# Attention and a mixture of experts on one core: the residual kept in the output, six weight groups and four output banks

## The chip, the cores and the metric

The kernel runs on one core of a Trainium2 chip. The metric is the time of one execution on the device, in microseconds (us). The core has five engines that work at the same time, each through its own list of instructions in order: PE (matrix products; its weight loads are shown as PEld), DVE (vector work), ACT (activation functions), POOL (general work and transfers that need more than a plain copy) and SP (which only issues transfers). SP, ACT and POOL each issue transfers on a queue of their own.

## The reference, cut to what matters

```python
x = x + layernorm(attn(layernorm(x)))        # 16 x 256 tokens, 256 wide, 16 heads of 128
x = x + layernorm(ffn(layernorm(x)))

def ffn(h):                                  # T = 4096 tokens, E = 64 experts, M = 176
    scores = softmax(h @ gate.T)             # 3 of 8 groups of experts, then 6 of 64 experts
    buf[expert, slot] = h[token]             # 96 slots for each expert; a token past slot 95 shares it
    out = (silu(buf @ Wg.T) * (buf @ Wu.T)) @ Wd.T       # for each expert
    y = sum over the 6 of out[expert, slot] * score
    return y + (silu(h @ Sg.T) * (h @ Su.T)) @ Sd.T      # the shared expert, 352 wide
```

All arithmetic is in float32. The first `x +` is the residual that this change is about: it is needed in attention and again at the very end.

## The kernel before, in words

Tokens lie in 32 chunks of 128, four chunks to a group of tokens (`CG`), so there are 8 groups of tokens. `SG0` is 4 and `G` is 5.

**Attention** (L89 to L697) walks over 16 batches and 16 heads; the work of one head is spread over several steps so that PE always has something to do. Behind it runs `route` (L400), a generator that is advanced by one piece per step: it normalises the attention's output, adds it to `xs` (L430), normalises again, finds the six experts of each token and scatters the token's row into `buf_d` in DRAM. `xs` holds the whole residual, 32 KB per partition, from the first load to the last instruction.

**The barrier** (L812 to L825): when attention ends, its memory goes to `EWB` = 5 weight groups. A weight group is four experts' `wg`, `wu` and `wd`, 2.1 MB. Meanwhile PE computes the shared expert of the first four groups of tokens (`shared_steps`), and the last `route` runs in between.

**The experts** (L950 to L989) follow an order written out by hand. In pass `e` PE turns rows for expert `e+2`, multiplies expert `e`, turns expert `e-1` and finishes expert `e-2` (`expert_out`, L890). ACT scales that result, and POOL adds it to one of three sums in DRAM (`y_ds`) by an accumulating scatter (L899). After each fourth expert ACT also copies one row of each result into `ol` (L906). SP refills weights (`load_group`, L787) and rows (`load_buf`, L839) expert by expert as slots come free, and later loads the first sums (`load_early`).

**The end** (L991 to L1079) goes over the 8 groups of tokens in the order `ends`. For each group:

- PE makes the overflow term and, for the last three groups of tokens, the shared expert's output, into two banks (`put_out`, L994); a bank is read by one DVE add (L1004).
- POOL adds the first two sums (`sum_two`, L1007), DVE adds the third (L1012) and takes statistics (L1016, L1017), ACT takes the root (L1022).
- `norm_out` (L1025): DVE makes reciprocal and `nb` (L1029, L1031), ACT normalises (L1033), POOL adds the residual from `xs` (L1034), SP stores (L1035).

`pieces` says in which of these passes PE makes which piece of the shared expert's inner layer (`shared_in`, L736); ACT and DVE finish a piece one pass later (`shared_act`, L747 and L748). The norm of a group is done in the next pass, ahead of that pass's adds.

Of the kernel before, what the change touches and what calls it, by code (L numbers as in the profile page):

```python
# [9 lines left out]
F32 = mybir.dt.float32  # L10
# [8 lines left out]
P = 128  # L19
# [21 lines left out]
EWB = 5  # L41
# [9 lines left out]
def block_kernel(ctx, tc, x, wq, sq, wk, sk, wv, sv, wo, so, bqk, bv, bo, gateT, wg, wu, wd, sgT, suT, sdT, out):  # L51
# [13 lines left out]
    xs = keep.tile([P, NC, D], F32, name="xs")  # L65
# [4 lines left out]
    make_identity(nc, ident)  # L70

# [17 lines left out]
    def attention(split):  # L89
# [9 lines left out]
        rt = None  # L99
        wp = ph1.enter_context(tc.tile_pool(name="wp" + nm_, bufs=1))  # L100
# [299 lines left out]
        def route(c0, n):  # L400
# [29 lines left out]
            nc.vector.tensor_add(x1, x1, a)  # L430
            yield
# [268 lines left out]
    def ffn(nm_, last_route, ph0):  # L700

        EN = mybir.EngineType
        ph2, ph3, ph4 = ExitStack(), ExitStack(), ExitStack()
        cp = ph2.enter_context(tc.tile_pool(name="cp2" + nm_, bufs=1, reuse_waits="tile"))
        ep = ph2.enter_context(tc.tile_pool(name="ep" + nm_, bufs=2, reuse_waits="tile"))
        ewp = ph3.enter_context(tc.tile_pool(name="ewp" + nm_, bufs=EWB, reuse_waits="tile"))
# [66 lines left out]

        def group_tile(name):

            return ewp.tile([P, EG * (2 * DC * M + 2 * D)], F32, tag="w", name=name)
# [35 lines left out]
        with tc.manual_schedule(engines={EN.PE, EN.DVE, EN.Activation, EN.SP}):  # L812
            load_h(0)
            load_h(1)
            for g in range(EWB):
                load_group(g)
            sh = shared_steps()
            for fill in BARRIER:
                for _ in range(fill):
                    next(sh)  # L820
                next(last_route, None)
            for _ in last_route:
                next(sh, None)
            for _ in sh:
                pass  # L825
        ph0.close()

        xp = ph4.enter_context(tc.tile_pool(name="xp" + nm_, bufs=2, side="right", reuse_waits="tile"))
        pst = ph4.enter_context(tc.tile_pool(name="pst" + nm_, bufs=2, side="right", space=PSUM, reuse_waits="tile"))

        def load_buf(g, j=None):

            if g not in bns:
                bns[g] = xp.tile([CAP, EG, RW], F32, tag="bn", name=f"bn{g}", bufs=5)
            rows = buf_d.rearrange("(g j c) d -> g c j d", j=EG, c=CAP)[g]
            if j is None:
                nc.gpsimd.dma_start(bns[g], rows)
            else:
                nc.sync.dma_start(bns[g][:, j], rows[:, j])  # L839
# [71 lines left out]
        pieces = {0: (G + 1, 1), 1: (G + 1, 2), 2: (G + 2, 0), 4: (G + 2, 1), 5: (G + 2, 2)}  # L911
# [3 lines left out]
        def place(t, at, g, i):  # L915

            ys.setdefault(g, {})[i] = t[:, at : at + Y].rearrange("p (c d) -> p c d", d=D)
# [8 lines left out]
        def load_early(k):  # L926

            if k < EWB:
                t = group_tile(f"y{k}")
                if k < 2:  # L930
                    for n in range(4):
                        place(t, n * Y, ends[4 * k + n], 2)
                        load_sum(ends[4 * k + n], 2)
                else:
                    for n in range(4):
                        place(t, n * Y, ends[2 * (k - 2) + n // 2], n % 2)
                load_ov(t, 4 * Y, ends[k])
                return

            for n in range(5):  # L940
                t = xp.tile([P, EG * RW], F32, tag="bn", name=f"yr{n}", bufs=5)
                if n == 0:
                    load_ov(t, 0, ends[5])
                    load_ov(t, V, ends[6])
                else:
                    place(t, 0, ends[6 + (n - 1) // 2], (n - 1) % 2)
            t = xp.tile([P, Y], F32, tag="ob", name="yo", bufs=3)
            load_ov(t, 0, ends[7])

        with tc.manual_schedule():  # L950
            for g in range(EWB):
                load_buf(g)
# [5 lines left out]
            for e in range(E + 2):  # L958
                g, j = e // EG, e % EG
                if e + 2 < E:  # L960
                    rows_turn(e + 2)
                if e < E:
                    sg, pg = expert_in(e)
                if e in (24, 32, 40):
                    shared_in(SG0, (e - 24) // 8)
                if 1 <= e <= E:
                    expert_turn(e - 1)
                if e < E:
                    expert_mul(e, sg, pg)
                if e in (25, 33, 41):  # L970
                    shared_act(SG0, (e - 25) // 8)
                    if e == 41:
                        load_h(G + 1)
                if e in (46, 54):
                    shared_put(SG0, (e - 46) // 4)
                if j == 2 and g + 1 < NG_:
                    slot_weights(g + 1)
                if e >= 2:
                    expert_out(e - 2)
                if e >= E:  # L980
                    shared_in(G, 0, (e - E,))

                g, j = divmod(e - 1, EG)
                if g >= 1:
                    if g + EWB - 1 < NG_:
                        load_buf(g + EWB - 1, j)
                        load_group(g + EWB - 1, j)
                    elif j == 0:
                        load_early(g + EWB - 1 - NG_)  # L989

            ph5 = ExitStack()  # L991
            yp = ph5.enter_context(tc.tile_pool(name="yp" + nm_, bufs=2, reuse_waits="tile"))

            def put_out(g, c):  # L994

                y = ys[g][2][:, c : c + 2, :]
                po = ps.tile([P, 2, D], F32, tag="o", name=f"ov{g}_{c}")
                for i in range(2):
                    if g > SG0:
                        shared_out(po[:, i, :], g, c + i, True, False)  # L1000
                    nc.tensor.matmul(  # L1001
                        po[:, i, :], lhsT=ovTs[g][:, (c + i) * P : (c + i + 1) * P], rhs=ol, start=g <= SG0, stop=True
                    )
                return lambda: nc.vector.tensor_tensor(y, y, po, ALU.add)  # L1004

            def sum_two(g):
                nc.gpsimd.tensor_add(ys[g][0], ys[g][0], ys[g][1])  # L1007

            def take_stats(g, c, n):

                y = ys[g][0][:, c : c + n, :]
                nc.vector.tensor_add(y, y, ys[g][2][:, c : c + n, :])  # L1012
                st = yp.tile([P, n, 6], F32, tag=f"st{n}", name=f"st{g}_{c}")
                mv = yp.tile([P, n, 2], F32, tag=f"mv{n}", name=f"mv{g}_{c}")
                for i in range(n):
                    nc.vector.bn_stats(st[:, i, :], y[:, i, :])  # L1016
                    nc.vector.bn_aggr(mv[:, i, :], st[:, i, :])  # L1017
                stat[g, c] = mv

            def take_root(g, c, n):  # L1020
                rs = yp.tile([P, n], F32, tag=f"rs{n}", name=f"rs{g}_{c}")
                nc.scalar.activation(rs, stat[g, c][:, :, 1], AF.Sqrt, bias=eps_t)  # L1022
                stat[g, c] = rs, stat[g, c]

            def norm_out(g, c, n, eng):  # L1025

                y = ys[g][0][:, c : c + n, :]
                rs, mv = stat.pop((g, c))
                nc.vector.reciprocal(rs, rs)  # L1029
                nb = yp.tile([P, n], F32, tag=f"nb{n}", name=f"nb{g}_{c}")  # L1030
                nc.vector.scalar_tensor_tensor(nb, mv[:, :, 0], -1.0, rs, ALU.mult, ALU.mult)  # L1031
                for i in range(n):
                    nc.scalar.activation(y[:, i, :], y[:, i, :], AF.Identity, bias=nb[:, i : i + 1], scale=rs[:, i : i + 1])  # L1033
                eng.tensor_add(y, y, xs[:, g * CG + c : g * CG + c + n, :])  # L1034
                nc.sync.dma_start(out_v[:, g * CG + c : g * CG + c + n, :], y)  # L1035

            load_early(EWB)
            nc.gpsimd.tensor_add(ys[SG0][2], ys[SG0][2], ss[SG0])
            for g in ends:
                for i in range(2):  # L1040
                    load_sum(g, i)
            shared_in(G, 1)
# [6 lines left out]
            sum_two(ends[0])  # L1049
            act, norm = (G + 1, 0), None  # L1050
            for n, g in enumerate(ends):
                tail = n + 1 == len(ends)
                add = [put_out(g, 0), put_out(g, 2)]
                if n in pieces:
                    shared_in(*pieces[n])
                if not tail:
                    sum_two(ends[n + 1])

                if norm is not None:
                    norm_out(norm, 0, CG, nc.gpsimd)  # L1060
                if tail:
                    break
                for f in add:
                    f()
                take_stats(g, 0, CG)
                if act:
                    shared_act(*act)
                act, norm = pieces.get(n), g
                take_root(g, 0, CG)
            for f, c in zip(add, (0, 2)):  # L1070
                f()
                take_stats(g, c, 2)
                take_root(g, c, 2)
            norm_out(g, 0, 2, nc.gpsimd)
            norm_out(g, 2, 2, nc.vector)
# [52 lines left out]
```

## Time and profile before

| | |
|---|---|
| runs | 1483.54 us median of three (1479.08 to 1484.61) |
| profiled execution | 1487.39 us; span from first to last instruction 1485.4 us; mean granted clock 0.980 |
| PE busy | 1435.0 us, 97% |
| DVE busy | 1112.6 us, 75% |
| ACT busy | 670.0 us, 45% |
| POOL busy | 372.0 us, 25% |
| transfers | 127.37 MB, 86 GB/s over the span |
| attention | to about 1131 us |
| barrier | to about 1203 us |
| experts | to about 1380 us |
| end | the rest |

Times in the text are us from the start of the span, if they have four digits before the point, and durations otherwise. A line such as "L1004 DVE" means the instructions of that line of the kernel on that engine. A matmul is listed with the shapes it writes and reads; the "clock" is the share of PE's full clock that was granted. "<-" in brackets behind an instruction is what ended the idle time before it.

### The profile page before, as it was taken

How to read it: one execution, taken by the hardware profiler on the slowest of the kernel's cores; microseconds unless marked ns; L12 is line 12 of the kernel's file. 1: busy time of each engine (PE TensorE's matmuls, PEld its weight loads, DVE VectorE, ACT ScalarE, POOL GpSimd, SP SyncE). 2: the span in 40 equal slices, each digit the busy share in tenths (PEclk: the TensorE clock that was granted, in tenths of full speed). 3: DMA queues.
4: the chain of work that ended last, by engine and by line, in shares of the span. 5: the costliest groups of instructions: out<-in, count | busy, mean ns of one | idle time of the engine just before them, and what ended most of it. 6: DMA issues, size and time to landing. Idle time of an engine off the chain costs nothing. (4 is left out here: it accounts for less than half of the span.)

```text
span 1485.4 us, 24839 instructions
## 1 busy us (share of the span) xinstructions
PE 1435.0 (97%) x8476; PEld 1213.2 (82%) x8476; DVE 1112.6 (75%) x3491; ACT 670.0 (45%) x1800; POOL 372.0 (25%) x334
## 2 busy tenths in 40 slices
PE   7999999999999999999999999999999998999994
PEld 4688999888989889898989898898886587788542
DVE  5878798878898987998898889879896233444463
ACT  4653463545455444635454554445454222223343
POOL 2420000320060015003200600150432424444652
PEclk9999999999999999999999999999999999999975
DMA  5246140410010101100010101000106859998731
GB/s 168 89 128 170 53 142 1 135 64 29 1 47 15 43 19 32 47 15 24 18 51 15 26 15 43 10 7 29 35 22 191 250 142 253 246 259 203 225 114 51
DMA packets 99850, 127.37 MB, mean 86 GB/s; under 512 B 15787, under 2 KB 82129, under 8 KB 99275
## 3 DMA queue, kind: packets, MB, share of 16 engines
q1 hardware_dynamic: 75587, 96.99, 21.9%
q0 software_dynamic: 18176, 17.07, 5.4%
q10 hardware_dynamic: 5952, 11.63, 2.4%
q8 instruction: 70, 1.15, 0.3%
q14 instruction: 65, 0.53, 0.1%
HBM read 81.98 MB, written 65.99 MB: 100 GB/s over the span
## 5 line engine op out<-in xcount | busy, mean ns | idle before, releaser
L327 ACT ACTIVATE pe<-sc,nms 128x256 f32<-128x256 f32 x512 | 239.8, 474 | 205.9 <-DVE nms L323 138.6
L583 POOL DMA_INDIRECT buf_d<-h,si x192 | 190.6, 993 | 508.5 <-DVE si L580 430.0
L352 PE MATMUL po<-pT,v 128*128 128x256 f32 x1024 | 276.4, 382 | 3.3 <-DVE oT L356 2.1
L319 PE MATMUL sc<-qk 128*128 128x256 f32 x1024 | 266.9, 381 | 1.3 <-ACT pT L343 0.7
L343 ACT COPY pT<-pt 128x512 f32<-128x512 f32 x256 | 150.2, 587 | 218.2 <-PE pt L341 217.6
L307 PE MATMUL pq<-xnT,wq 128*128 128x256 f32 x1024 | 215.7, 325 | 0.6 <-DVE wq L191 0.4
L352 PEld LDWEIGHTS po<-pT,v 128*128 128x128 f32 x1024 | 175.7, 190 | 23.2 <-ACT pT L343 3.5
L319 PEld LDWEIGHTS sc<-qk 128*128 128x128 f32 x1024 | 174.9, 190 | 17.9 <-issue 2.3
L312 DVE TENSOR_TENSOR qk<-pq,bqk_t 128x512 f32<-128x512 f32 x256 | 174.7, 683 | 12.2 <-PE pq L307 10.9
L321 DVE TENSOR_REDUCE nm<-sc 128x2 f32<-128x512 f32 x256 | 174.7, 683 | 11.7 <-PE sc L319 9.2
L341 PE MATMUL pt<-ident,pe 128*128 128x128 f32 x1024 | 171.1, 277 | 2.1 <-DVE pe L333 1.0
L307 PE MATMUL pq<-xnT,wk 128*128 128x256 f32 x1024 | 171.4, 286 | 0.4 <-DVE wk L191 0.4
L333 DVE TENSOR_SCALAR pe<-pe,rsum 128x256 f32<-128x256 f32 x512 | 167.9, 370 | 1.2
L307 PEld LDWEIGHTS pq<-xnT,wq 128*128 128x128 f32 x1024 | 156.6, 191 | 14.5 <-issue 1.5
L292 PE MATMUL pv<-wv,xnT 128*128 128x512 f32 x512 | 164.0, 442 | 2.7 <-POOL wv L195 2.5
L341 PEld LDWEIGHTS pt<-ident,pe 128*128 128x128 f32 x1024 | 125.6, 141 | 44.9 <-issue 8.2
L354 DVE TENSOR_SCALAR oT<-po,bv_t 128x256 fp32r<-128x256 f32 x256 | 122.7, 479 | 51.8 <-PE po L352 49.5
L307 PEld LDWEIGHTS pq<-xnT,wk 128*128 128x128 f32 x1024 | 141.1, 189 | 2.3 <-DVE wk L191 1.1
L371 PE MATMUL pp<-wo,oT 128*128 128x256 f32 x1024 | 132.5, 286 | 0.0
L371 PEld LDWEIGHTS pp<-wo,oT 128*128 128x128 f32 x1024 | 125.2, 189 | 0.8
L356 DVE SCALAR_TENSOR_TENSOR oT<-po,bv_t,oT 128x256 fp32r<-128x256 f32 x256 | 122.1, 477 | 2.7
L899 POOL DMA_INDIRECT y_d<-ob,tok x64 | 91.3, 1426 | 111.2 <-ACT ob L898 43.6
(214 smaller groups left out, 1830.5 us busy)
## 6 DMA issues: line engine op xcount, KB each, us to landing
y<-y_d SPq DMA_DIRECT2D x20, 512.0 KB
y_d<-zero SPq DMA_DIRECT2D x2, 4096.0 KB
w<-wg SPq DMA_DIRECT2D x44, 176.0 KB
w<-wu SPq DMA_DIRECT2D x44, 176.0 KB
w<-wd SPq DMA_DIRECT2D x44, 176.0 KB
buf_d<-empty SPq DMA_DIRECT2D x1, 6528.0 KB
bn<-buf_d SPq DMA_DIRECT2D x44, 102.0 KB
hs<-hT_d ACTq DMA_DIRECT2D x8, 512.0 KB
```

What stands on the lines that cost most here:

```text
L292: nc.tensor.matmul(pv, lhsT=x[:, dc, c * P : (c + 1) * P], rhs=ws["wv", j][:, dc, :], start=i == 0, stop=i == len(terms) - 1,)
L307: nc.tensor.matmul(pq[:, m, :], lhsT=w[:, dc, o : o + HD], rhs=x[:, dc, :], start=i == 0, stop=i == len(terms) - 1,)
L312: marks[0:] = [nc.vector.tensor_tensor(qk, pq, bqk_t[:, h, :].unsqueeze(2).to_broadcast([P, 2, S]), ALU.add)]
L319: nc.tensor.matmul(sc[:, c, :], lhsT=qk[:, 0, c * P : (c + 1) * P], rhs=qk[:, 1, :], start=True, stop=True)
L321: nc.vector.tensor_reduce(nm, sc, AX.X, ALU.max, negate=True)
L327: nc.scalar.activation(pe[:, c, :], sc[:, c, :], AF.Exp, bias=nms[:, c : c + 1], scale=SC, accum_out=ssum[:, c : c + 1])
L333: nc.vector.tensor_scalar_mul(pe[:, c, :], pe[:, c, :], rs[:, c : c + 1])
L341: nc.tensor.transpose(pt[:, kc, c * P : (c + 1) * P], pe[:, c, kc * P : (kc + 1) * P], ident)
L343: nc.scalar.copy(pT[b, h], pt)
L352: nc.tensor.matmul(po, lhsT=v[:, kc, o : o + HD], rhs=t[:, kc, :], start=kc == 0, stop=kc == 1)
L371: nc.tensor.matmul(pp, lhsT=x[:, h, c * P : (c + 1) * P], rhs=ws["wo", h // HPG][:, h % HPG, :], start=i == 0, stop=i == len(terms) - 1,)
L583: ins = nc.gpsimd.indirect_dma_start(out=buf_d[:, :], out_offset=bass.IndirectOffsetOnAxis(ap=si[:, c, k : k + 1], axis=0), in_=h[:, c, :] ...
```

## The change

- `xs` lives only as long as attention and routing. `route` stores the residual into the output as soon as it is made, on SP's queue. In the end, the normalised group is added to the output in DRAM by an accumulating transfer of POOL's queue (seven of them); the last group's residual is loaded back (`xl`) and added as before.
- With the memory that this leaves there are six weight groups, the sixth in a pool of its own that is opened after the barrier. `load_early` also takes six tiles.
- `load_buf` loads a whole weight group's rows in one transfer on ACT's queue, instead of four transfers on SP's.
- `put_out` writes its two halves into banks of two pools (`ps` and `pso`), two deep each; the bank pair of `pst` is given up for it after the experts.
- In passes 1, 3 and 5 of the end (`direct`) POOL adds all three sums, and DVE adds the banks to that; the others are as before. `pieces` moves the last two pieces one pass forward.
- `nb` is made by two instructions, the second of them on POOL.

```diff
-EWB = 5
+EWB = 6
...
-    xs = keep.tile([P, NC, D], F32, name="xs")
...
+    def behind_stored(ins, g):
+        for s in stored[g].values():
+            tc.add_manual_dep(ins.ins, s.ins.name, ...)
...
+        xs = rc.tile([P, NC, D], F32, name="xs")
...
             nc.vector.tensor_add(x1, x1, a)
+            stored.setdefault(g, {})[c0] = nc.sync.dma_start(out_v[:, c0 : c0 + n, :], x1)
...
-        ewp = ph3.enter_context(tc.tile_pool(name="ewp" + nm_, bufs=EWB, reuse_waits="tile"))
+        ewp = ph3.enter_context(tc.tile_pool(name="ewp" + nm_, bufs=EWB - 1, reuse_waits="tile"))
...
-            for g in range(EWB):
+            for g in range(EWB - 1):
                 load_group(g)
...
         ph0.close()
+        ewp2 = ph3.enter_context(tc.tile_pool(name="ewp2" + nm_, bufs=1, reuse_waits="tile"))
...
-        pieces = {0: (G + 1, 1), 1: (G + 1, 2), 2: (G + 2, 0), 4: (G + 2, 1), 5: (G + 2, 2)}
+        pieces = {0: (G + 1, 1), 1: (G + 1, 2), 2: (G + 2, 0), 3: (G + 2, 1), 4: (G + 2, 2)}
+        direct = (1, 3, 5)
...
-            for g in range(EWB):
-                load_buf(g)
+            for g in range(5):
+                load_buf(g, nc.gpsimd)
+            load_group(EWB - 1)
...
                 if g >= 1:
+                    if j == 0 and g + 4 < NG_:
+                        load_buf(g + 4, nc.scalar)
                     if g + EWB - 1 < NG_:
-                        load_buf(g + EWB - 1, j)
                         load_group(g + EWB - 1, j)
...
+            pso = ph7.enter_context(tc.tile_pool(name="pso" + nm_, bufs=2, side="right", space=PSUM, reuse_waits="tile"))
...
-                y = ys[g][2][:, c : c + 2, :]
-                po = ps.tile([P, 2, D], F32, tag="o", name=f"ov{g}_{c}")
+                y = ys[g][0 if n in direct else 2][:, c : c + 2, :]
+                po = (pso if c else ps).tile([P, 2, D], F32, tag="o", name=f"ov{g}_{c}")
...
+            def sum_y(n):
+                y = ys[ends[n]]
+                nc.gpsimd.tensor_add(y[0], y[0], y[1])
+                if n in direct:
+                    nc.gpsimd.tensor_add(y[0], y[0], y[2])
...
-                nc.vector.scalar_tensor_tensor(nb, mv[:, :, 0], -1.0, rs, ALU.mult, ALU.mult)
+                nc.vector.tensor_scalar(nb, rs, -1.0, None, ALU.mult)
+                eng.tensor_tensor(nb, nb, mv[:, :, 0], ALU.mult)
...
-                eng.tensor_add(y, y, xs[:, g * CG + c : g * CG + c + n, :])
-                nc.sync.dma_start(out_v[:, g * CG + c : g * CG + c + n, :], y)
...
+                if n:
+                    norm(n - 1, 0, CG, nc.gpsimd)
+                if n + 1 < nt:
+                    sum_y(n + 1)
+                if n:
+                    h = ends[n - 1]
+                    behind_stored(
+                        nc.gpsimd.dma_start(out_v[:, h * CG : (h + 1) * CG, :], ys[h][0], accum_op=ALU.add), h
+                    )
```

## The prediction

> **What bounds the kernel now.** I read the engine table and the 40 slices first, then the chain that ended last, then windows of 10 us over the end, then the timeline of single engines where a window showed PE idle or its clock down. PE is busy 97% of the span. The slices show where it is not, and where it is busy at a lower clock:
>
> ```profile
> PE   7999999999999999999999999999999998999994
> PEclk9999999999999999999999999999999999999975
> DMA  5246140410010101100010101000106859998731
> ```
>
> Up to slice 30 there is attention, with PE full. Slices 33 to 37 are the experts: PE drops to 8 in slice 34, and the DMA engines are at 90% or more from there to slice 36. In the last two slices the clock falls. Windows over the end, with PE's busy time, the granted clock and the DMA share:
>
> ```profile
> 1410.00:1420.00 10.00, 7.52 (x25) 4.24 (x24) 8.47 (x22) 6.42 (x10) 7.79 (x4) 1.00 0.98 318
> 1420.00:1430.00 10.00, 9.28 (x19) 5.78 (x20) 6.37 (x16) 7.61 (x12) 5.58 (x4) 0.51 0.19 62
> 1430.00:1440.00 10.00, 10.00 (x18) 5.12 (x18) 2.95 (x7) 0.00 (x0) 3.95 (x2) 0.50 0.16 52
> 1460.00:1470.00 10.00, 10.00 (x22) 6.12 (x21) 2.48 (x6) 1.15 (x3) 2.34 (x1) 0.50 0.16 56
> ```
>
> From 1420.4 to 1440.4 and from 1451 to 1471.4 PE runs at half clock, so the end is slow matmuls, not DMA. PE's timeline shows what comes before each drop:
>
> ```profile
> 1415.53 1.99 PE L1001 MATMUL ov<-ol,y 64*128 64x256 f32 x8
> 1420.72 2.93 PE L752 MATMUL ov<-sd_t,aT 128*128 128x256 f32 x6 [3.21 <-DVE y L1004]
> 1436.75 3.78 PE L736 MATMUL sp<-hs,sg_t 128*128 128x512 f32 x4
> 1452.53 2.08 PE L752 MATMUL ov<-sd_t,aT 128*128 128x256 f32 x4 [2.71 <-DVE y L1004]
> 1457.29 1.22 PE L752 MATMUL ov<-sd_t,aT 96*128 96x256 f32 x2 [2.68 <-DVE aT L748]
> 1470.45 1.13 PE L1001 MATMUL ov<-ol,yo 64*128 64x256 f32 x2
> ```
>
> Twice PE waits for the add at L1004, because the two banks that `put_out` writes are read only there, and once for the last piece of `aT`. Call the passes over `ends` turns 0 to 7. A turn's cycle, from the chain in time order:
>
> ```profile
> 1413.62 0.60 DVE y L1004
> ...
> 1414.31 1.24 DVE y L1012
> ...
> 1419.17 0.31 ACT rs L1022
> ...
> 1419.50 0.19 DVE rs L1029
> ...
> 1419.99 0.69 DVE y L1004
> ```
>
> DVE adds the banks (1.3 us), adds the third sum (L1012, 1.24), takes statistics (2.1), waits for ACT's table load and root (1.6), then takes reciprocal and `nb` (0.5): turn 2 starts at 1412.95 and turn 3 at 1419.99, 7.04 us apart. Lastly, the experts:
>
> ```profile
> 1249.54 0.58 ACTq L906 DMA_DIRECT2D ol<-ob  x1
> 1250.22 0.31 ACT L875 ACTIVATE sg<-pg 96x176 f32<-96x176 f32 x1 [5.04 <-DMA w<-wu]
> ```
>
> ACT's instruction before L906 ended at 1245.2, so it stands there 4.4 us, although the weights in use were requested by 1163.2, 86 us earlier. In the compiled program the transfers of SP and ACT are counted on eight semaphores in turn, and a transfer is issued only when the one eight places earlier has landed; at L906 that is a `wu` load of the group being fetched. PE idles 0.44, 2.61 and 2.09 us in the three windows of 20 us from 1220 on, and the clock of 0.91 in the third costs another 1.8: about 7 us.
>
> **The change part by part.**
>
> *Four banks, and pieces (G+2, 1), (G+2, 2) in turns 3 and 4.* At full clock `put_out` of a shared group took 8.4 us (1397.99 to 1406.37), of another 1.9, one `shared_in` piece 3.6. With a second pair of banks PE no longer waits at 1417.5, where turn 3's `put_out` ends: it runs the piece to 1421.1 and turn 4's `put_out` to 1429.5, at full clock, since the pause before the drop is gone. Before, that ended at 1436.75. Turn 4's add ends at 1430.2, and 1.24 + 2.1 + 1.6 + 0.5 later, at 1435.7, turn 5's begins (before: 1443.47).
>
> What is late next is the last `aT`. In turn 5 ACT normalises turn 4 (2.08, from about 1436.0), loads the table (1.28) and does Silu (0.6), to 1440.0; DVE multiplies (0.65), to 1440.7. PE has by then done its piece (1433.1), turns 5 and 6 (1436.9) and four matmuls of turn 7; it idles about 3 us. So the last third of turn 7's first chunk starts at 1440.8, not 1457.29: 16.5 us earlier. I assume that this pause drops the clock, as 3.2 and 2.7 us did, and that it stays down to the end, as in the trace: the rest then takes the same 14.3 us (1457.29 to 1471.58), and everything behind moves by 16.5. At full clock it would take 7.2 us; DVE then sets the end, whose second add could start near 1450.0 instead of 1471.62: 21.6 us gained.
>
> In the trace the clock stays at 0.50 for 20 us while PE is busy nearly all the time; it returns at 1440.4, 3.6 us after the 512-column L736 begin, and in the experts it was down for 4 us only (1262.4 to 1266.3). [...]
>
> *Direct turns 1, 3, 5.* L1012 falls away (1.24 us of DVE each) and POOL does a second add (2.34 to 3.34). POOL's turn is then 0.2 + 2 x 2.4 to 3.3 + 0.8, that is 5.8 to 7.6 us, against a turn of ACT of 2.08 + 1.28 + 0.6 + 1.28 + 0.3 + 0.9 = 6.4. Turn 1 is held by PE's 1406.37 as before; its statistics end at 1409.4 and turn 2 starts at 1411.4 instead of 1412.95. Turns 4 and 7 wait for PE, so this is inside the sum already; if POOL slips, turn 5 has 5 us of room (its sums can be done by 1430).
>
> *`nb` split.* L1031 took 0.16 us alone and 1.95 beside a POOL add. Now DVE does the scalar part and POOL the product, behind POOL's second add. A POOL add of 128x512 took 1.26 and of 128x1024 2.34, so 128x4 is about 0.2; with the handoff +0.4 us in the last turn, 0 to +2.
>
> *Residual by accumulating transfer.* POOL loses its 2.34 us adds and gains seven issues; L445, 512 KB, took 0.80 us there. How long 512 KB with an add take no row shows: a plain `out` store filled the DMA engines for about 1.6 us, and the scatters of 96 rows came 4.2 to 5 us apart on one sum at the end of the experts, their 1.4 us issue included. 512 rows are 5.3 times as many: from 1.6 us (as a store) to 5.3 x 2.8 = 15 us each. I take 5, since part of the 2.8 is one round trip and not rows. The seventh is issued near 1450 and lands before 1469; at 15 us they queue up (7 x 15 from 1408), to 1513 at worst. [...]
>
> *Stores of x1 and the load back.* Nine stores (4 MB) on SP's queue in attention, where the DMA share is mostly 0.1: nothing, if SP stands no longer than the adds before it. Behind them on SP wait the code checks, fetched 16 us ahead, so a store without that cover costs at most its own 1.6 us, 14 for all nine; I take 0. The last store is queued behind `w4`, and the rows `bn0` lie where `xs` lay: issued at 1182.8 and landing 5.6 to 8.6 us later, they are needed at 1201.8, so 10 us of room. The load `xl` (0.5 MB) comes 30 us before use.
>
> *Sixth group, rows from ACT's queue.* The sixth group doesn't remove the wait at L906, which is for a transfer in flight, not for weights in use. Twelve weight loads, one row load and one `ol` per group stand where there were seventeen, so eight places reach back about as many bytes. `slot_weights` and PE are behind ACT if it stands at the row load. Gain 7 at best, and a cost by the worst stalls below; I take 0. Loading `w5` at about 1180 falls into a DMA share of 0.7.
>
> **Sum.** The profiled execution took 1487.39 us (span 1485.4 and 2.0 around it). -16.5 + 0.4 = -16.1 gives 1471.3. The median of the runs lies 3.85 below it; carried over, 1467.
>
> **The rivals.** 0.5%, about 7.4 us, is what a measurement here can tell from no change.
> - *Clock kept in turn 7*: the pause is shorter than 2.6 us, as at 1248.4 where the clock held. 1487.39 - 21.2 - 3.85 = 1462. With the stall at L906 gone as well, 1455. For it: PE's queue is full until 1437. Against: Silu of the last piece stands behind turn 4's normalisation.
> - *Clock lost before turn 4 as well*, if the piece in turn 3 has to wait for its banks (turn 2's multiply): turn 4's add returns to 1436.9, half the gain goes, 1475; or the accumulating transfers take over 10 us each and their queue ends the kernel near 1480.
> - *Slower: ACT stands at every row load.* Place: the load before L906's successor, eleven times. Price: the worst two stalls cost PE about 3.4 us each. From the fifth on the gain is gone, from the seventh the kernel is slower by over 0.5%, and with all eleven it is 1467 + 37 = 1504. For it: DMA share 1.0 from 1220 to 1360. Against: the awaited transfer is no later than L906's own.
> - *The change does not do what it says*: six groups and a queue of their own for the rows remove no wait; with the banks and pieces failing too, 1483. I hold the first half of this to be so, and it is in the sum as 0.
>
> **Chances.** Forecast 0.55; clock kept 0.15; half the gain or accumulation as the end 0.15; slower 0.15. Faster by over 0.5% (below 1476.1): 0.55 + 0.15 + a part of the third = 0.73; within: 0.12; slower: 0.15. Range 1457 to 1482: it takes in clock kept with a part of the L906 stall, and both forms of the third case; left out are the slower case and a little below. The forecast's own range is 1461 to 1474.
>
> **What will show it.** Right: PE without a pause between 1392 and 1436 and clock 1.0 there; turn 4's `put_out` in 8.4 us; the last pause before an `aT` multiply; L906 late as before; POOL's accumulate issues near 0.8 us. Wrong: ACT waiting in front of the row loads, a chain that ends in an accumulating transfer, the clock down in turn 4, or PE idle beyond 5.1 us among the experts.

## The result, and the profile after

The changed kernel took 1471.56 us in the median of seven runs (1470.15 to 1477.40), the kernel before 1484.61 us in seven runs beside it (1476.24 to 1485.88): a ratio of 0.9935, 95% interval 0.9908 to 0.9962. The forecast was 1467 us, faster than before; measured are 4.6 us more than that, and 13 us less than before in the medians. The profiled execution took 1477.35 us, with a span of 1475.5 us and a mean clock of 0.985. In what follows L numbers are those of the changed kernel unless a variant of the kernel before is named: L747 `shared_in`, L758 and L759 `shared_act`, L763 `shared_out`, L780 the store of a shared sum, L886 and L909 ACT's two steps of an expert, L850 the row load, L917 `ol`, L1005 and L1008 `put_out` and its add, L1082 the accumulating transfers.

The 40 slices of the changed kernel, for the same three rows as before:

```profile
PE   7999999999999999999999999999999999999995
PEclk9899999999999999999999999999999999999996
DMA  5246140240011101101010001001013979999594
```

PE has no 8 any more in slice 34, and the clock is lost only in the last slice (6 instead of 7 and 5 in two). The 8 in the second slice of the clock is new; it comes back below. Windows of 10 us over the end (busy time of PE, PEld, DVE, ACT and POOL with their instruction counts, then granted clock, DMA share and GB/s):

```profile
1410.00:1420.00 10.00, 10.00 (x30) 4.98 (x30) 6.98 (x17) 9.18 (x14) 7.48 (x5) 1.00 1.11 321
1420.00:1430.00 10.00, 10.00 (x34) 5.55 (x32) 6.64 (x23) 7.36 (x11) 6.92 (x5) 1.00 1.11 249
1430.00:1440.00 10.00, 10.00 (x34) 5.58 (x34) 5.51 (x14) 4.66 (x7) 6.08 (x4) 1.00 0.58 80
1440.00:1450.00 10.00, 6.86 (x22) 4.37 (x21) 6.85 (x18) 8.47 (x14) 6.09 (x5) 0.81 0.45 62
1450.00:1460.00 10.00, 10.00 (x21) 5.85 (x21) 6.13 (x17) 2.68 (x7) 2.99 (x4) 0.50 0.53 64
```

From 1410 to 1440 PE is full at clock 1.00, where before it stood still and then ran 20 us at 0.51. What is left is the pause and the half clock of turn 7. PE's timeline there:

```profile
1426.48 1.46 PE L763 MATMUL ov<-sd_t,aT 128*128 128x256 f32 x6
...
1434.23 0.70 PE L1005 MATMUL ov<-ol,y 64*128 64x256 f32 x2
...
1442.11 1.13 PE L763 MATMUL ov<-sd_t,aT 128*128 128x256 f32 x4
1446.37 1.22 PE L763 MATMUL ov<-sd_t,aT 96*128 96x256 f32 x2 [3.14 <-DVE aT L759]
...
1459.54 1.22 PE L1005 MATMUL ov<-ol,yv 64*128 64x256 f32 x2
```

Turn 4's `put_out` takes 8.4 us (1426.48 to 1434.9; before, 16.0). Then PE waits 3.14 us for the last `aT`, and the rest of turn 7 takes 14.4 us at half clock.

The stages of the two profiled executions, cut at the barrier's first shared matmul, the first `pg` of the experts and the start of expert 63's last row of matmuls, add up to the whole difference:

| | before | after | difference |
|---|---|---|---|
| attention, to | 1131.73 | 1135.89 | +4.16 |
| barrier | 71.08 | 71.47 | +0.39 |
| experts | 176.75 | 177.69 | +0.94 |
| end | 105.84 | 90.45 | -15.39 |
| span | 1485.4 | 1475.5 | -9.9 |

The attention's 4.16 us come from one stretch at half clock, from 60.5 to 70.7 us (4.66 us lost there, 0.5 won elsewhere); it isn't in this execution of the kernel before. Pauses of PE are alike in both there (0.97 and 0.55 us within two microseconds after; 0.94 and 0.55 before). Among all executions profiled in this study it appears in three of eight of the changed kernel and its variants, and in none of five of the kernel before and its variants. That is too few to say whether it belongs to the change. The profiled execution is 5.8 us longer than the median.

The first four experiments ran on one chip, the next four on another, the last three on the first again. In the last seven all times were longer (the kernel before 1659 to 1677 us: in attention PE stood before single transpositions for up to 21 us, whatever the kernel; the reason was not found), so each is compared with the kernel before beside it, and by its stages. The changed kernel itself was run again only beside the second four, so what is said of the last three against it goes through the kernel before.

### The profile page after: what moved, and what is told of

Its sections match the earlier page's. It is cut to its first block, busy times and chain, and to the rows that moved or that the text cites. A ratio compares the mean times of both kernels' runs of the same rounds, so it can differ in the third digit from the quotient of the medians.

```text
span 1475.5 us, 24749 instructions
## 1 busy us (share of the span) xinstructions
PE 1428.8 (97%) x8476; PEld 1208.6 (82%) x8476; DVE 1108.1 (75%) x3489; ACT 670.8 (45%) x1800; POOL 370.2 (25%) x345
## 5 line engine op out<-in xcount | busy, mean ns | idle before, releaser
L328 PEld LDWEIGHTS sc<-qk 128*128 128x128 f32 x1024 | 175.5, 190 | 18.5 <-issue 2.5
```

The lines of the kernel that those rows point to most:

```text
L328: nc.tensor.matmul(sc[:, c, :], lhsT=qk[:, 0, c * P : (c + 1) * P], rhs=qk[:, 1, :], start=True, stop=True)
```

## The experiments

The theory: the gain is made in the end, by banks and pieces that keep PE busy, so that its clock stays up. The rivals: the direct turns and the adds taken from POOL make it; or the six groups and the queues do. The second question was what the prediction had put at nothing: the wait of ACT at its own transfers.

**One part at a time.** Three variants of the kernel before and one of the changed kernel.

```diff
 banks_only   + po = (pso if c else ps).tile(...)          (pst closed after the experts)
 pieces_only  + pieces = {..., 3: (G + 2, 1), 4: (G + 2, 2)}
 banks_pieces   both
 after_two_banks: the changed kernel with  po = ps.tile(...)
```

banks_only: 

> The kernel before with four banks for put_out and nothing else of the change (pieces (G+2, 1) and (G+2, 2) stay in turns 4 and 5). Theory (the end is gained by keeping PE busy, so that its clock stays up): no pause at 1417, put_out of turn 4 in 8.4 us at clock 1.0, but Silu of the last piece stands in turn 6, a turn later than in the changed kernel, so the last aT comes about 3 us later than there: 12 to 14 us faster than before, with a longer pause ahead of the last third of turn 7. Rival (the direct sums and the residual taken off POOL bring the gain): under 4 us faster. Rival (the banks are nothing without the pieces): no change.

pieces_only: 

> The kernel before with the pieces (G+2, 1) and (G+2, 2) in turns 3 and 4 instead of 4 and 5, and two banks as before. Theory: the piece in turn 3 fills the 3.2 us in which PE waited for the add, so turn 4's put_out starts near 1421 and takes 8.4 us at clock 1.0; later put_out of turns 6 and 7 wait for the adds of turns 5 and 6 with two banks, so the first chunk of turn 7 starts 3 to 6 us later than with four banks: 9 to 13 us faster than before. Rival (the pause is there with the piece as well, and the clock drops): within 3 us of before.

banks_pieces: 

> The kernel before with four banks and the new pieces; no sixth group, rows on SP's queue, residual from xs by POOL, no direct turn. Theory: all of the gain of the end is here, 15 to 17 us from expert 63 to the end, and the whole is 15 to 17 us faster than before, that is 1 to 4 us faster than the changed kernel, which loses some 1.5 us at the first experts. Rival (the direct sums, or the adds that POOL loses, are needed for it): the turns grow, under 10 us faster than before.

after_two_banks: 

> The changed kernel with put_out on two banks only (all of it in ps). Theory: as pieces_only, with a turn shortened by the direct sums (1.24 us less of DVE in turns 1, 3 and 5) and some 1.5 us lost at the first experts: 8 to 13 us faster than before, 2 to 5 us slower than the changed kernel. Rival (buffers and queues bring the gain, banks nothing): as fast as the changed kernel, 13 us faster than before. Rival (without the banks nothing is left): as before.

Measured beside the kernel before at 1481.82 us:

| | median, us | ratio, 95% | end in the profiled execution, us |
|---|---|---|---|
| banks_only | 1477.29 | 0.9960 (0.9935 to 0.9985) | 93.6 |
| pieces_only | 1476.39 | 0.9965 (0.9946 to 0.9984) | 90.8 |
| banks_pieces | 1468.58 | 0.9910 (0.9880 to 0.9940) | 89.0 |
| after_two_banks | 1477.61 | 0.9968 (0.9946 to 0.9991) | 92.2 |

Banks and pieces together are 13.2 us faster than before, as much as the whole change, with nothing else of it; the whole change with two banks is only 4.2 us faster. So the theory holds: these two make the gain, each alone a third or so of it, and in the sum six groups, queues, accumulating transfers and direct turns add nothing that these runs can tell from zero (smaller gains and losses among them may cancel). The sizes were forecast too high: 12 to 14 and 9 to 13 us for one alone, against 4.5 and 5.4; 15 to 17 for both, against 13.2; 8 to 13 for the change with two banks, against 4.2. Each of the two alone leaves its own wait late in the end. banks_only, PE's timeline (its last `aT` comes a turn later):

```profile
1438.95 0.70 PE L752 MATMUL ov<-sd_t,aT 128*128 128x256 f32 x2 [1.79 <-DVE aT L748]
1445.99 1.22 PE L752 MATMUL ov<-sd_t,aT 96*128 96x256 f32 x2 [6.34 <-DVE aT L748]
```

pieces_only (turns 6 and 7 wait for the adds that empty their two banks):

```profile
1441.77 3.43 PE L1001 MATMUL ov<-ol,yr 64*128 64x256 f32 x8 [1.51 <-DVE y L1004]
1448.82 2.93 PE L752 MATMUL ov<-sd_t,aT 128*128 128x256 f32 x6 [3.62 <-DVE y L1004]
```

These waits explain 2 to 5 us of the profiled ends. The rest of the 8 us between the medians isn't in the profiled executions of the two, which were faster than their medians (1473.60 and 1474.72 us); what the other executions lost can't be read from them and stays open.

**The changed kernel again.** 

> The changed kernel once more, beside its variants. Theory (the clock drop at 60 us and the 1.5 us lost at the first experts belong to the program): both are there again, and it is about 13 us faster than before. Rival (the drop at 60 us was chance): the clock is 1.0 from 40 to 100 us, and the first shared matmul of the barrier starts some 4 us earlier.

Measured: 1665.65 us beside 1676.61, ratio 0.9934 (0.9909 to 0.9959). It is the same gain, and the experts again take longer than the 176.75 us of before (178.97); but the same experts in the three variants of the kernel before took 175.5 to 178.5 us, so a difference of one or two microseconds there is within what executions differ by. The clock was 1.00 from 40 to 100 us, so the drop at 60 us isn't fixed to the program.

**The last Silu a turn earlier.** Turn 5 normalises turn 4's group and loads a table before Silu of the last piece. In the changed kernel's timeline ACT and DVE show that this is not needed:

```profile
1439.30 1.28 ACT L1032 ACT_TABLE_LOAD   x1 [4.71 <-DVE mv L1026]
...
1443.71 1.28 ACT L758 ACT_TABLE_LOAD   x1
...
1445.63 0.68 DVE L759 TENSOR_TENSOR aT<-ssg,sp 96x512 f32<-96x512 f32 x1 [1.00 <-ACT ssg L758]
```

ACT stands idle for 4.71 us before turn 4's root, and its last table is that of Silu; the piece is there at 1438.5.

```diff
                 act = pieces.get(n)
+                if act == (G + 2, 2):
+                    shared_act(*act)
+                    act = None
                 take_root(n, 0, CG)
```

> The changed kernel with Silu and multiply of the last piece (G+2, 2) issued in turn 4, ahead of its root, instead of turn 5. Theory (the pause before the last aT costs the clock): ACT stands idle there and has the Silu table loaded, so aT is ready near 1440.5, no pause of over 2 us is left before turn 7's last third, the clock stays at 1.0 to the last matmul, PE's rest of turn 7 takes 7.2 us, and DVE sets the end: 6 to 8 us faster than the changed kernel. Rival (the clock falls whatever the pause, because of the form of the matmuls): only the pause of 3.1 us is gained. Rival (DVE's turn is the bound): under 2 us gained.

Measured: 1660.99 us, 0.9915 (0.9887 to 0.9942), 4.7 us faster than the changed kernel beside it in the medians; the end took 83.9 instead of 88.4 us. The variant's timeline:

```profile
1625.66 0.59 ACT L758 ACTIVATE ssg<-sp 96x512 f32<-96x512 f32 x1 [2.44 <-PE sp L747]
...
1630.85 1.56 PE L763 MATMUL ov<-sd_t,aT 128*128 128x256 f32 x6
...
1642.82 0.65 DVE L1008 TENSOR_TENSOR y<-y,ov 128x512 f32<-128x512 f32 x1
```

Windows in turn 7 (columns as above), first of the changed kernel beside it, then of this variant:

```profile
1636.00:1646.00 10.00, 9.84 (x20) 5.69 (x20) 8.18 (x19) 4.83 (x10) 3.99 (x4) 0.50 0.74 103
```

```profile
1630.00:1640.00 10.00, 9.40 (x37) 5.88 (x35) 8.72 (x24) 4.49 (x10) 7.11 (x5) 1.00 0.58 75
```

Turn 7 runs through without a pause (x6 in one row), the clock stays at 1.00 to the last matmul, and from the first `ov` to the last PE needs 52.6 us instead of 60.7. Of these 8.1 us 3.6 are given back: the second add starts 3.4 us after PE's last matmul, since DVE comes late to it. So the pause cost the clock, as the theory has it; the matmuls are the same, so their form alone doesn't. It isn't one lucky execution either: of the thirteen profiled in this study the three with this order (the other two are best_changed and best_before below) kept the clock at 1.00 through turn 7, and in the other ten it fell in turn 7 or just ahead of it. The forecast of 6 to 8 us was a little high, as DVE takes over as the bound earlier than I had worked out.

**ACT without transfers among the experts.** The stall that the prediction had put down to the transfer eight places back is there in the changed kernel at the same place, L917, with the row load behind it:

```profile
1243.77 0.61 ACTq L917 DMA_DIRECT2D ol<-ob  x1
1245.34 0.32 ACTq L850 DMA_DIRECT2D bn<-buf_d  x1
1245.76 0.31 ACT L886 ACTIVATE sg<-pg 96x176 f32<-96x176 f32 x1 [4.56 <-DMA w<-wu]
```

The landings in the traces bear it out: the `wd` load eight places ahead of this `ol`, issued at 1237.74, lands completely at 1243.69, 0.08 us before `ol` is issued; for the row load it is a `wu` load that lands at 1245.27, and for L906 in the kernel before one that lands at 1249.46, 0.08 us before the issue at 1249.54. The traces also show the count of eight: SP's and ACT's transfers, 380 in the kernel before and 341 in the changed one, share eight semaphores, and of the 372 and 333 that had another ahead of them on theirs none was issued before that one had landed completely (142 and 118 were issued within 0.2 us of the landing).

```diff
-                        load_buf(g + 4, nc.scalar)
+                        load_buf(g + 4, nc.sync)
...
-                nc.scalar.dma_start(ol[g * EG : (g + 1) * EG, :], ...)
+                nc.gpsimd.dma_start(ol[g * EG : (g + 1) * EG, :], ...)
```

> The changed kernel with the rows loaded from SP's queue (as one transfer per group, as in the changed kernel) and ol stored from GpSimd's queue, so that ACT issues no transfer among the experts. Theory (ACT stands at its transfers for one eight places back, and PE and DVE stand behind ACT): no stall of ACT of 3 to 5 us at an issue is left between 1220 and 1380, PE's idle time there falls from 3.9 us to under 1 us and the clock stays up: 3 to 6 us faster than the changed kernel. Rival (the weights themselves are late, the DMA share being 1.0): the stall turns up at the matmuls as a wait for w, and the time stays.

Measured: 1663.24 us, 0.9922 (0.9897 to 0.9947), 2.4 us faster than the changed kernel in the medians where 3 to 6 were forecast. The experts took 172.3 us instead of 179.0, that is 6.6 us less. One window of each, first the changed kernel run beside it, then this one (PE's busy time, clock, DMA share, GB/s):

```profile
1430.00:1450.00 20.00, 15.83 (x99) 0.96 1.02 259
```

```profile
1430.00:1450.00 20.00, 20.00 (x135) 1.00 1.02 254
```

PE's 4.2 us of idle time in this window are gone at the same DMA share, so the weights weren't late: the engine that issued was. Rows and `ol` were moved together, so the share of each isn't separated. But the end took 96.9 instead of 88.4 us. This variant's timeline shows why:

```profile
1576.46 1.06 POOL L917 DMA_DIRECT2D ol<-ob  x1
...
1582.81 3.19 PE L1005 MATMUL ov<-ol,y 64*128 64x256 f32 x8 [2.42 <-DMA ol<-ob]
```

On POOL's queue the last `ol` stands behind the last scatters; PE waits 2.42 us for it, and the clock falls for 6.8 us there. In turn 7 the half clock lasts 13.65 us in this execution and 10.24 in the other; half of that difference, some 1.7 us by estimate, comes on top.

**The sixth group later.**

```diff
-            load_group(EWB - 1)
...
+                if g == 0:
+                    load_group(EWB - 1, j)
```

> The changed kernel with the sixth weight group loaded expert by expert during the first group of experts, not ahead of them. Theory (the load of 2.1 MB at 1188 delays the transfers of the shared experts' sums and ACT's copies at the first experts): experts 0 to 2 lose no more than in the kernel before, 1 to 2 us faster than the changed kernel; the sixth group brings nothing by being early. Rival (the sixth group's lead is what the rest of the experts live on): PE waits for w in groups 5 to 8, slower than the changed kernel by some us.

Measured: 1679.80 us, 1.0023 (1.0005 to 1.0041): 14 us slower than the changed kernel. The forecast failed, and so did the rival, since PE waits for no weights in groups 5 to 8 (the experts take 174.1 us, less than the 179.0 beside it). But the edit did not make the load later, as it was meant to: it began at 1372.8, in the changed kernel at 1374.9, now in twelve transfers instead of three. So the theory about its time remains untested. The loss is in the barrier, 88.4 instead of 71.2 us:

```profile
1386.66 1.08 ACT L758 ACTIVATE ssg<-sp 128x512 f32<-128x512 f32 x2 [16.16 <-DMA w<-wu]
1387.31 3.78 PE L747 MATMUL sp<-hs,sg_t 128*128 128x512 f32 x4 [17.18 <-ACT ssg L758]
```

SP has no work among the experts in front of these loads, so it issued the twelve at 1372.8 to 1383.0, still in the barrier. In the compiled program they stand ahead of ACT's second store L780 in the count of eight; the load eight places ahead of it landed at 1386.16 and it was issued at 1386.23, where the changed kernel beside it issued it at 1371.56. It is the mechanism of the slower rival, at a place that the prediction did not name.

**No direct turn.** `direct = ()` in the changed kernel.

> The changed kernel with no direct turn (DVE adds the third sum in every turn, POOL does one add). Theory (turns 4 and 7 wait for PE, so 1.24 us of DVE in turns 1, 3 and 5 are not on the path): within 2 us of the changed kernel, 11 to 14 us faster than before. Rival (the direct turns shorten the end): 3 to 4 us slower than the changed kernel. Rival (POOL's second add delays its nb product): faster than the changed kernel by up to 2 us.

Measured: 1652.15 us beside 1659.24, 0.9959 (0.9936 to 0.9982), 7 us faster than before instead of the forecast 11 to 14; the interval still overlaps that of the changed kernel (0.9909 to 0.9959). Its end took 92.0 us. In turn 5, DVE and PE:

```profile
1617.27 2.44 DVE L1021 TENSOR_TENSOR y<-y,y 128x1024 f32<-128x1024 f32 x1
...
1621.88 0.65 DVE L759 TENSOR_TENSOR aT<-ssg,sp 96x512 f32<-96x512 f32 x1
...
1622.59 1.22 PE L763 MATMUL ov<-sd_t,aT 96*128 96x256 f32 x2 [4.70 <-DVE aT L759]
```

The third sum's add, 2.44 us beside a POOL add, stands in front of the multiply that makes the last `aT`. PE's pause grows from 3.14 to 4.70 us, so in this place the direct turn 5 is worth 1.6 us, and the half clock behind the pause lasted to the last matmul here.

**Both findings together,** in the changed kernel and in the kernel before. The last group's `ol` stays on ACT, the other fifteen go from POOL:

```diff
+                q = nc.gpsimd if g + 1 < NG_ else nc.scalar
+                q.dma_start(ol[g * EG : (g + 1) * EG, :], obs[g][CAP - 1 : CAP, :, :])
```

best_changed (rows on SP's queue as well): 

> The changed kernel with both findings: Silu of the last piece in turn 4, and no transfer issued by ACT among the experts except the last group's ol (the other fifteen from GpSimd's queue, the rows from SP's). Theory (the two gains lie in different stages and add up; the last ol is in time again from ACT): experts near 172 us from the first pg to expert 63's last matmul, the end near 84 us, together 10 to 12 us faster than the changed kernel, 19 to 24 us faster than before. Rival (with the experts faster, the sums of the end are loaded late or PE waits at the end): the end takes 88 us or more, under 17 us faster than before.

best_before: 

> The kernel before with four banks, the new pieces, Silu of the last piece in turn 4, and fifteen of the sixteen ol stores from GpSimd's queue; five weight groups, rows from SP, residual from xs, no direct turn. Theory (the sixth group, the accumulating transfers and the direct sums are not needed for any of the gain): as fast as the same version of the changed kernel within 4 us, 19 to 25 us faster than before. Rival (the sixth group, or the rest of the change, is needed once the stalls are gone): PE waits for w in the experts, or POOL's adds hold DVE in the end: 5 us or more slower than the same version of the changed kernel.

Measured beside the kernel before at 1659.24 us: best_changed 1639.81, 0.9898 (0.9869 to 0.9927), 19.4 us faster, with 171.5 us of experts and 84.7 of the end; best_before 1644.31, 0.9916 (0.9892 to 0.9940), 14.9 us faster, with 174.2 and 88.2. Both gains are there, each in its stage, and best_changed has the largest gain of this study in the medians (its interval overlaps that of banks_pieces). best_before is 4.5 us behind, between the theory's 4 and the rival's 5, and its 14.9 us fall short of the forecast 19 to 25. In the profiled executions 2.7 us of the difference are the experts, and they are one more place of the same wait, the load of `hs` in pass 41, the only transfer that ACT issues in the middle of the experts (the load eight places ahead of it lands at 1492.78; best_before's timeline):

```profile
1492.80 0.33 ACTq L728 DMA_DIRECT2D hs<-hT_d  x1
1493.18 0.47 ACT L898 ACTIVATE ob<-eo,wc 96x256 f32<-96x256 f32 x1 [5.71 <-DMA w<-wg]
...
1494.36 0.34 PE L886 MATMUL ap<-ident,prod 96*88 96x96 f32 x2 [2.94 <-DVE eq L845]
```

best_changed has the same load, with one row load per group on SP where this one has four and with a sixth group, and PE has no idle time around it; which of the two matters was not tested. The other 3.5 us are the end. There POOL still adds the residual, and DVE's adds beside it are slower: 2.88 us in turn 4 and 1.86 us in turn 7 for adds that take 1.23 and 0.69 in best_changed. It looks as if this part of the change pays once PE is no longer the bound; no run changes it alone.

## Why the prediction was right, step by step

**Four banks and pieces: right, to the size, in the profiled executions.** From the first `ov` to the last third of turn 7's first chunk it took 64.75 us before and 48.34 after, 16.4 less (forecast 16.5). `put_out` of turn 4 in 8.4 us, a pause of 3.14 us (forecast 3), and 14.4 us behind it at half clock (forecast 14.3): all as worked out. In the medians banks_pieces shows 13.2: the profiled execution of the kernel before was one of the longer ones, with two stretches of 20.48 us at half clock in its end.

**The clock that stays down: right here, by luck in part.** In the changed kernel's profiled execution it stayed down to the end. In its second one it came back after 10.2 us, before the last chunk. The stretch of 20 us was one draw of several lengths, not a fixed one (see the last section, whose times also replace the 4 us that the prediction read for the drop among the experts: it was 3.41). The rival with the clock kept needed another order of ACT, not a shorter draw: silu_same shows it.

**Direct turns: a value missed.** I held that turns 4 and 7 wait for PE, so that the 1.24 us in turns 1, 3 and 5 count for nothing of their own. Turn 7 waits for DVE's multiply, and without the direct turn 5 that is 1.6 us later. The sum was right since it worked with the direct order. POOL's turn is 6.2 to 7.2 us, as forecast.

**The split `nb`.** POOL's part takes 0.20 us as forecast. From PE's last matmul to the end it is 14.74 us instead of 13.82, +0.9, where +0.4 was in the sum; what of it is `nb` was not separated, so no run shows the 0.4 of the sum by itself.

**Accumulating transfers: off the end, two sizes off.** The seven issues and their landing:

```profile
L1082 POOL DMA_DIRECT2D out<-y x7: 1285/1293/1389, 1412.3 to 1457.1; - x7
...
DMA to landing us min/median/max: 5.8/6.3/10.2
```

The first row gives minimum, median and maximum of the issue in ns, 1.29 us where 0.80 was forecast from a plain transfer; the second the landing, 6.3 us against 5. The last is issued at 1457.1 and lands before the stores of 1466.5, so neither size reached the end. That part of such a time is not rows, as the forecast of 5 assumed, the trace of the kernel before shows for plain transfers: 4 KB of `ol` (L906) took 2.27 us from issue to landing at the shortest, 512 KB of `out` (L1035) 2.90.

**Stores of x1.** Forecast 0. best_changed and best_before, neither with a drop at 60 us, reach the barrier at 1308.57 and 1307.43 us: 1.1 us apart, less than variants of the changed kernel differ among themselves beside each other (1322.85 to 1324.68).

**The sixth group: right that it removes no wait, but the price of its load was left out.** The wait at `ol` stayed (4.56 us at 1245.76), and the row load behind it cost ACT at most another 1.1 us, not 3.4: the slower rival's price was too high because the row load follows `ol` directly, and what it awaits lands soon after. I noted that `w5` falls into a DMA share of 0.7 and gave that no price. ACT's last two copies of a shared sum (L778) began 10.7 us after the store before them (1198.30 to 1208.96), where before it was 5.7 us; in the second execution of the changed kernel the profile names the landing of that store as what they waited for (9.17 us), beside the load of `w5`. Expert 2's `sg` came 1.5 us later (5.75 us behind the first `pg`, 4.29 before), in the second execution 1.7. What else made the experts' +0.94 wasn't separated from the spread of 175.5 to 178.5 us that the same experts showed in variants of the kernel before. That `w5` is what delays the store was not tested alone; w5_late shows that the same load, otherwise divided, can cost 17 us.

**The sum.** -16.1 was forecast for the profiled execution and -10.0 came. The end gave -15.4; the +0.9 of the experts, +0.4 of the barrier and +4.2 of the half clock in attention were in no term. In the medians it is -13.05; whether the half clock at 60 us was in those executions isn't on record.

## What to carry to other kernels

A short wait of PE costs more than itself when the clock falls behind it (here 3 us of waiting were followed by 10 to 14 us at half clock), so look for what PE could do in that gap (a piece from a later pass, another pair of banks) before shortening the engine it waits for; and then for the next gap, since here two changes gave 13 us together and about 5 each. When a compute engine issues transfers, its work stands behind them: if they are counted with another queue's in a few semaphores, each issue can wait for that queue's bulk loads (here ACT stood 4.56 us at one `ol` and the row load behind it), and it is cheaper on an engine on which nothing urgent is queued (the experts took 6.6 us less with ACT's issues moved), but not where its own data is the next thing needed (PE then waited 2.42 us for the last `ol`).

## What the runs showed of the hardware

**The half clock comes in multiples of 3.41 us.** In windows of 0.1 us its begin and end can be read to some hundredths:

| execution | from, to (us) | length | of 3.41 |
|---|---|---|---|
| before, experts | 1263.16, 1266.57 | 3.41 | 1 |
| off_act, first `ov` | 1583.39, 1590.21 | 6.83 | 2 |
| after, attention | 60.49, 70.73 | 10.24 | 3 |
| banks_only, turn 7 | 1441.29, 1454.95 | 13.65 | 4 |
| after_two_banks, turn 7 | 1442.81, 1459.88 | 17.07 | 5 |
| before, turn 4 | 1420.17, 1440.65 | 20.48 | 6 |

The lengths are one to six times 3.4133 us, to a hundredth of a microsecond. In each of the thirteen profiled executions all changes of the clock lie on one grid of 3.4133 us, to 0.001 us, and where the grid lies differs from execution to execution. A busy window of this grid did not always bring the clock back: PE is listed as busy for all 19.00 us from 1421 to 1440 in the kernel before, at a clock of 0.50, and it took six windows. The stretches among the experts lasted one window in every execution, those of the end one to six. What keeps it down was not found.

**A pause's length alone doesn't decide; PE's idle time within one window of the grid does, for the most part.** PE's clock fell after a pause of 1.51 us at 1441.77 in pieces_only, while it stayed up through 1.79 us at 1437 in banks_only. The first pause lay in one window; of the second 0.72 us lay in one window and the rest in the next, at whose end the clock did fall, with the next pause begun. Cut along its grid, the executions together have 5398 windows at full clock. After none of the 5163 with less than 1.0 us of idle time did the clock fall, after all 121 with more than 1.93 us it did, and after 13 of the 114 in between (idle time from the profile, whose ends of matmuls are modelled, so the bounds are rough). The drop at 60 us is such a case in between, the kernel before first, then the changed kernel with the window behind:

```profile
58.31:61.72 3.41, 1.95 (x9) 1.22 (x9) 3.07 (x5) 1.41 (x6) 2.14 (x2) 1.00 0.32 87
```

```profile
57.07:60.49 3.42, 1.90 (x10) 1.17 (x9) 3.42 (x8) 1.42 (x4) 2.55 (x2) 1.00 0.21 39
60.49:63.90 3.41, 3.41 (x11) 2.41 (x10) 1.71 (x6) 1.96 (x6) 0.80 (x1) 0.50 0.38 120
```

PE is idle for 1.5 us in both first windows, and only the second loses the clock. So executions of one kernel differ: 29 of the kernel before, beside the first four experiments, took 1475.23 to 1490.15 us, at a mean clock of 0.988 in the shortest and 0.977 in the longest.
